# One-hot routing rows made by three instructions per group over pairs of 16-bit elements, with the late routing steps moved, in a recurrent layer followed by a mixture of experts

## The chip, the cores and the metric

The kernel runs on one core of one Trainium2 chip. The metric is the device time of one execution in microseconds. A core has a matrix engine (TensorE, "PE" in the profile, its weight loads "PEld"), a vector engine (VectorE, "DVE"), a scalar engine (ScalarE, "ACT"), a general engine (GpSimd, "POOL", which here also issues the gathers and scatters), and a queue engine (SyncE, "SP", which issues most plain DMAs). Each engine works through its own instructions in order and waits for the others through semaphores.

## The reference, cut to what matters

```python
# x: (2, 1024, 256), cond: (2, 256)
xW = einsum('ntd,dh->nth', x, Wx) + b
next_h = tanh(xw_t + prev_h @ Wh)              # scanned over 1024 tokens, from h = cond
...
logits = h_flat @ gate_w.T                     # 2048 tokens, 8 experts
top_v, top_i = top_k(logits, 2)                # two experts for each token
probs  = softmax(top_v)
...
hidden = silu(h @ wg_e.T) * (h @ wu_e.T)       # for each expert e
out   += combine[e] * (hidden @ wd_e.T)        # weights of the tokens that chose e
return x + out
```

The reference applies every expert to every token and multiplies by a weight that is zero for six of the eight. The kernel computes each expert only on the tokens that chose it, so it has to build, on the chip, a table that says which token stands in which place of which expert's list.

## The kernel before

**Three stages.** A recurrent stage (the loop over `s` from 8 to 63, L605) computes the hidden states. It cuts each of the two sequences into 64 chunks of 16 tokens and runs all 128 chunks side by side, each from 40 steps ahead of its first token; `df` holds by how much a chunk's start differs from the end of the chunk before, and a slower path (not taken here) is there for when that is too much. Steps 48 to 63 are the chunks' own tokens: each of them makes one tile of 128 tokens final. A routing stage runs inside the last steps of the recurrence and the first steps of the experts. An expert stage then takes ten units of work (an expert, or a part of an expert's tokens), each in eight steps. An expert step has a `front` (12 matrix products into `pgu_t`, L713), a `gate` (a Silu on ACT, then on DVE a product `g`, L721, then on ACT a copy `hh`, L732, and on DVE a remainder `hl`, L733, which lies beside `hh` in the same tile for a unit of 256 columns), and a `back` (products with `wd`, L875) for the step two before.

**Routing.** The 16 tiles are taken in four groups of four (`groups`; g0 to g3 below). For a group:

- `route_tile` (L333): for each tile, PE transposes the state and forms the logits (L340), and ACT copies them to `rows`.
- `route_max` (L343): for each tile, DVE finds the largest logits and their places (MAX8, then an index search).
- `route_choice` (L349): for the group, DVE makes `oh`, `sel` and `dl`, what was chosen and the difference of the two logits.
- `route_exp`: ACT takes an exponential of `dl`. It stands on ACT's queue in program order, so a tanh of the recurrence behind it waits with it.
- `route_position` (L376): PE counts, with `sel` of all groups so far, the place of each token in its expert's list (into `pos_ps`, L385).
- `route_code` (L389): DVE turns each of the eight (token, choice) columns of the group into a place: `v` is the block of 128 places, `m` the place inside it. POOL multiplies the probabilities in between.
- `route_onehot` (L413): DVE makes, for each of the eight columns, two rows of 128 values in 16-bit floats: `bv`, which holds the token's number (plus one) at column `v` and zero elsewhere, and `am`, which holds one at column `m`. Each row is one TENSOR_SCALAR instruction with a pointer to a scalar per partition (two pointers for `bv`): 16 instructions a group. The profile names both tiles `wd`, whose space they borrow, and gives their line as L50, the helper that keeps an engine's instructions in program order.
- `route_slots` (L422): PE multiplies `am` by `bv` and adds over all groups into `inv_ps`: the table of slots (L426).

`early_slots` (L459) reads the first two columns of the table once g0 and g1 are in, and POOL gathers two tiles of tokens for the first unit (from `rows_e`). `early_turn` transposes them on PE (L193), ACT makes `xhi`, DVE makes `xlo`, and the first front can start. `all_slots` (L471) reads the whole table once all groups are in, and POOL gathers two further tiles (the late gathers, from `rows_d`) for the second unit. They are turned in the expert step n = 6.

**What sets the order.** `at(step, f)` files a piece of work under a step, and `run(step)` emits all that is filed up to it, sorted by step and then by the order of filing. In the recurrence, `run(s - 0.5)` stands between the two halves of the eight products of step s, and `run(s)` at its end, after the tanh of ACT and after `seed(s + 2)`, which copies a summand to the accumulator of step s + 2 (one half on DVE, one on ACT in these steps). In expert step n, `run(64 + n + 0.15)` stands after the front, `+ 0.3` after the gate and `+ 0.6` after the back. `vec`, `act` and `pool` and all instructions of PE keep program order. `gated` and `halves` use `nc.vector` directly, and the compiler's planner may place those among the others.

In this listing the steps before stand in L542 to L583: the one-hot rows of g0 at 55 and 56, of g1 at 59, those of g2 and g3 split over 64.12 to 65.3; slots of g0 at 58, of g1 at 60.9, of g2 at 67.6, of g3 at 68.1; `early_slots` at 60.95 and `all_slots` at 68.15. A tile's maxima come one step after the tile.

Of the kernel before, what the change touches and what calls it, by code (L numbers as in the profile page):

```python
# [8 lines left out]
F32 = mybir.dt.float32  # L9
F32R = mybir.dt.float32r  # L10
F16 = mybir.dt.float16
I32 = mybir.dt.int32
U32 = mybir.dt.uint32
AF = mybir.ActivationFunctionType
ALU = mybir.AluOpType
# [4 lines left out]
P = 128  # L20
D = 256
NT = 2048
L = 16
R = 16
E = 8
# [7 lines left out]
ROW = D + E  # L33
S0 = 8
S16 = 28
GRP = 4
# [17 lines left out]
def rnn_moe(ctx, tc, xT, xrows, h0T, Wx, Wh, b, gw, W, out):  # L54
    nc = tc.nc
    pe = tc.keep_in_program_order
    vec, act, pool = (InOrder(tc, e) for e in (nc.vector, nc.scalar, nc.gpsimd))

    cst = ctx.enter_context(tc.tile_pool(name="cst", bufs=1))
    dram = ctx.enter_context(tc.tile_pool(name="dram", bufs=1, space=DRAM))  # L60
    ov = ctx.enter_context(tc.tile_pool(name="ov", bufs=1))
# [9 lines left out]
    iota_f = cst.tile([P, P], F32, name="iota_f")  # L71
    part_i = cst.tile([P, R], I32, name="part_i")
    tokp1 = cst.tile([P, R], F32, name="tokp1")
    iota16 = cst.tile([P, P], F16, name="iota16")
    trash = cst.tile([P, E * SPE // MT, MT], F32, name="trash").rearrange("p a b -> p (a b)")
    trash_i = cst.tile([P, E * SPE // MT, MT], I32, name="trash_i")
# [10 lines left out]
    def constants(part):  # L87
        if part == 0:
            vec.tensor_copy(iota_f, iota_i)
            vec.tensor_copy(tokp1, part_i)  # L90
            vec.tensor_scalar(ident, iota_f, 1.0, tokp1[:, 0:1], ALU.add, ALU.is_equal)
        elif part == 1:
            vec.tensor_scalar(upper, iota_f, 1.0, tokp1[:, 0:1], ALU.add, ALU.is_gt)
            vec.tensor_copy(ig[:, 0, 0:P], ident)
            vec.tensor_copy(ig[:, 1, E : P + E], ident)
            vec.tensor_copy(iota16, iota_f)
        elif part == 2:
            vec.tensor_copy(trash, trash_i.rearrange("p a b -> p (a b)"))
            vec.memset(ones16, 1.0)
            vec.tensor_scalar(base, iota_f[:, 0:E], float(SPE), None, ALU.mult)  # L100
        else:

            vec.tensor_scalar(keyc, iota_f[:, 0:E], FIRST - 0.5, 2.0**17, ALU.is_lt, ALU.mult)
            vec.scalar_tensor_tensor(keyc, iota_f[:, 0:E], float(8 * P * SPE + 1), keyc, ALU.mult, ALU.add)
# [15 lines left out]
    rt = wctx.enter_context(tc.tile_pool(name="rt", bufs=2))  # L120
# [24 lines left out]
    def flat(t):  # L145
        return t.rearrange("p a c -> p (a c)")
# [29 lines left out]
    hall = [flat(t).bitcast(F32).rearrange("p (r c) -> p r c", r=R) for t in early["gu_g"]]  # L176
# [25 lines left out]
    rp = c1.enter_context(tc.tile_pool(name="rp", bufs=1))  # L202
# [7 lines left out]
    zl = cst.tile([P, P], F32, name="zl")  # L210
    warm = rt.tile([P, 1], F32, name="warm")
# [10 lines left out]
    for c in range(4):  # L222
        constants(c)
# [31 lines left out]
    def bq(t):  # L255
        return t.rearrange("p (b q) -> p b q", b=2)
# [60 lines left out]
    slots = ov.tile([P, NO * NS], F32, name="slots")  # L317
# [6 lines left out]
    groups = []  # L324
    for g in range(R // GRP):
        o = (g % 2) * 4 * GRP * P
        gr = {"r0": g * GRP, "n": GRP}
# [61 lines left out]
    def route_code(gr, between=iter(())):  # L389
        n = gr["n"]  # L390
        rows = route_rows(gr, between)
        tmp = rt.tile([P, n, 2, E], F32, name="tmp")
        next(rows)
        vec.tensor_tensor(tmp, gr["oh"], pos_ps[:, 0:n, :].unsqueeze(2).to_broadcast([P, n, 2, E]), ALU.mult)
        code = rt.tile([P, n, 2], F32, name="code")
        next(rows)
        vec.tensor_reduce(code, tmp, AX.X, ALU.add)
        next(rows)
        big = 1.5 * 2.0**23 * P
        vv = rt.tile([P, n, 2], F32, name="vv")  # L400
        vec.tensor_scalar(vv, code, 0.5 - P / 2, big, ALU.add, ALU.add)
        next(rows, None)
        gr["v"] = v = rt.tile([P, 2 * n], F32, name="v")
        vec.tensor_scalar(v, vv.rearrange("p i c -> p (i c)"), -big, 1.0 / P, ALU.add, ALU.mult)
        gr["m"] = m = rt.tile([P, 2 * n], F32, name="m")
        next(rows, None)
        vec.scalar_tensor_tensor(m, v, -float(P), code.rearrange("p i c -> p (i c)"), ALU.mult, ALU.add)
        if gr["r0"] + n == NA:

            vec.tensor_scalar(gap, pos_ps[:, n, 0:1], -1.0 / P, float(ET), ALU.mult, ALU.add)  # L410
            vec.tensor_scalar(base[:, 0:1], gap, 0.0, None, ALU.max)

    def route_onehot(gr, part, js=range(2 * GRP)):  # L413

        for j in js:
            if part == 0:
                r = gr["r0"] + j // 2
                vec.tensor_scalar(gr["bv"][:, j, :], iota16, gr["v"][:, j : j + 1], tokp1[:, r : r + 1], ALU.is_equal, ALU.mult)
            else:
                vec.tensor_scalar(gr["am"][:, j, :], iota16, gr["m"][:, j : j + 1], None, ALU.is_equal)  # L420

    def route_slots(gr, i):  # L422
        for c in range(2):
# [90 lines left out]
    def first_weights(c, o):  # L514
# [6 lines left out]
            act.copy(hi[:, cc], raw[:, cc])  # L521
        (pool if c == 0 else vec).tensor_tensor(lo[:, cc], raw[:, cc], hi[:, cc].bitcast(F32), ALU.subtract)

    todo = {}

    def at(step, f, *args):
        todo.setdefault(step, []).append(lambda: f(*args))
# [12 lines left out]
    at(40, thresholds)  # L540

    for g, gr in enumerate(groups):  # L542
        t0 = 48 + gr["r0"] + gr["n"]
        for r in range(gr["r0"], gr["r0"] + gr["n"]):
            at(r + 49, route_tile, gr, r)
            at(min(r + 50, 64), route_max, gr, r)
        if g == R // GRP - 1:

            before = groups[g - 1]
            at(64, route_choice, gr)  # L550
            at(64.1, route_exp, gr)
            at(64.1, act.activation, warm, zl[:, 0:1], AF.Silu)
            at(64, rows_out, gr, ((0, P), (P + E, ROW)))
            at(64.12, route_position, gr)
            at(64.12, route_onehot, before, 0, range(4))
            at(64.12, route_code, gr, iter([lambda j=j: route_onehot(before, 0, range(j, j + 2)) for j in (4, 6)]))
            at(64.12, rows_out, gr, ((P, P + E),))
            at(64.3, route_onehot, before, 1)
            at(65.15, route_onehot, gr, 0)
            at(65.3, route_onehot, gr, 1)  # L560
            for i in range(gr["n"]):
                at(67.6, route_slots, before, i)
            for i in range(gr["n"]):
                at(68.1, route_slots, gr, i)
            continue
        at(t0 + 1, route_choice, gr)
        at(t0 + (1.5, 1.5, 1.9)[g], route_exp, gr)
        at(t0 + (2, 2, 2.5)[g], route_position, gr)
        at(t0 + (2, 2, 2.5)[g], route_code, gr)
        at(t0 + 1.5, rows_out, gr, ((0, P), (P + E, ROW)))  # L570
        at(t0 + (2, 2, 2.5)[g], rows_out, gr, ((P, P + E),))
        if g == 2:
            continue
        at(t0 + 3, route_onehot, gr, 0)
        at((t0 + 4, t0 + 3)[g], route_onehot, gr, 1)
        for i in range(gr["n"]):
            at(t0 + (6, 4.9)[g], route_slots, gr, i)
    at(60.95, early_slots)
    at(64, early_turn, 0)
    at(64, early_turn, 1)  # L580
    at(56, early_rows, 0, nc.sync)
    at(64.9, early_rows, 1, act)
    at(68.15, all_slots)  # L583

    inj = {}
    for s, q in ((15, 2), (31, 1), (47, 0)):
        t = rp.tile([P, 2, 2, 64], F16 if s + 1 < S16 else F32, name=f"inj{s}")
        inj[s] = (t, q)
        if q:
            nc.gpsimd.memset(t[:, :, :, 0:q], 0.0)  # L590
        for k in range(2):
            nc.gpsimd.tensor_copy(t[:, k, :, q], h0[:, k, :])
# [12 lines left out]
    for s in range(S0, 64):  # L605
# [7 lines left out]
        n, late = (s - S0 + 3) // 2, None  # L613
# [11 lines left out]
        if s in inj:  # L625
            t, q = inj[s]
# [4 lines left out]
        else:  # L631
            half = s + 1 < S16
            t = hp.tile([P, 2, 2, 64], F16 if half else F32, name="h16" if half else "h32")
# [4 lines left out]
        for j in range(2):  # L638
            x = bq(xw[s // 2][:, j, s % 2, :])[:, :, 0 : 64 - q0] if s == S0 else bq(acc[s % 2][j])[:, :, q0:64]
# [9 lines left out]
        n = (s - S0 + 6) // 2  # L649
# [1 line left out]
            x_split(n, (s - S0) % 2, act)  # L651
        run(s)

    df = ov.tile([P, 2, 2, 63], F32, name="df")
    for k in range(2):
        vec.tensor_tensor(df[:, k], inj[47][0][:, k, :, 1:64], bq(hall[k][:, L - 1, :])[:, :, 0:63], ALU.subtract)
    c1.close()

    okm = ov.tile([P, 1], F32, name="okm")
# [43 lines left out]
    with ExitStack() as c2:  # L703
# [216 lines left out]
        for n in range(len(steps)):  # L920
            i, s = steps[n]
            u = units[i]
            j = jobs.index(u.job)
            m = s + (NIC if i and units[i - 1].job is u.job else 0)
# [14 lines left out]
            if (j, m) in split_at:  # L939
                to, p = split_at.pop((j, m))  # L940
# [8 lines left out]
            if 2 <= n < len(steps) - NIC + TAIL + 2:  # L949
                v, t = done[n - 2]  # L950
# [180 lines left out]
```

## Time and profile before

| what | us |
|---|---|
| median of 3 runs | 395.32 (394.47 to 397.45) |
| the profiled execution, its own time | 392.31 |
| its span, first to last instruction | 390.5 |
| PE busy / PE weight loads busy | 371.0 / 349.5 |
| DVE / ACT / POOL busy | 232.5 / 200.5 / 119.9 |
| recurrence step 56 begins (PE) | 63.17 |
| first expert front begins (PE) | 81.11 |
| front of expert step 7 begins (PE) | 98.44 |

The granted clock of PE is 0.992 of full speed on average. Times inside the trace count from the start of the span. A line of the chain or of the timeline gives the start, the duration, the engine and the tile; "x8" means eight instructions merged. A line of the waits gives who waited for whom, the total in microseconds, how often, and the longest. A line of the groups gives busy time and the mean of one in nanoseconds, from issue to end: consecutive instructions overlap, so their starts lie closer together than that mean.

### The profile page before, as it was taken

How to read it: one execution, taken by the hardware profiler on the slowest of the kernel's cores; microseconds unless marked ns; L12 is line 12 of the kernel's file. 1: busy time of each engine (PE TensorE's matmuls, PEld its weight loads, DVE VectorE, ACT ScalarE, POOL GpSimd, SP SyncE). 2: the span in 40 equal slices, each digit the busy share in tenths (PEclk: the TensorE clock that was granted, in tenths of full speed). 3: DMA queues.
4: the chain of work that ended last, by engine and by line, in shares of the span. 5: the costliest groups of instructions: out<-in, count | busy, mean ns of one | idle time of the engine just before them, and what ended most of it. 6: DMA issues, size and time to landing. Idle time of an engine off the chain costs nothing.

```text
span 390.5 us, 7319 instructions
## 1 busy us (share of the span) xinstructions
PE 371.0 (95%) x2715; PEld 349.5 (90%) x2715; DVE 232.5 (60%) x619; ACT 200.5 (51%) x461; POOL 119.9 (31%) x124
## 2 busy tenths in 40 slices
PE   8899999988999999999999999999999999999990
PEld 7897898978998889999999999999989999999890
DVE  6676748988776565575537654575546656744410
ACT  3756666654664543665446553564454555535420
POOL 3790000213572501763041612432040015007041
PEclk9999999999999999999999999999999999999996
DMA  7943334441475343485233444345323307003122
GB/s 211 460 194 107 107 110 112 126 127 34 143 195 164 55 123 123 104 251 148 74 77 53 144 117 135 39 135 136 110 27 112 107 0 160 1 2 41 12 29 30
DMA packets 19291, 43.31 MB, mean 111 GB/s; under 512 B 4832, under 2 KB 14208, under 8 KB 16096
## 3 DMA queue, kind: packets, MB, share of 16 engines
q1 hardware_dynamic: 12432, 32.86, 25.2%
q0 software_dynamic: 6496, 9.09, 13.7%
q10 hardware_dynamic: 320, 0.80, 0.7%
q8 instruction: 24, 0.39, 0.4%
q14 instruction: 19, 0.16, 0.1%
HBM read 36.23 MB, written 10.22 MB: 119 GB/s over the span
## 4 chain that ended last, share of the span: by engine, by line
PE 82%; DVE 5%; DMA 4%; ACT 3%; POOL 2%; issue 2%; POOLq 0%; DVEq 0%
PE pgu_t L713 45%; PE yb L875 22%; PE pgu_t L612 8%; DVE wd L50 2%; PE ptr L286 2%; PE ptr L193 2%; POOL out_dram L454 2%; DMA gu_u<-in_xT_dram 1%; DMA wx<-in_Wx_dram 1%; PE pgu_t L875 1%; PE ptr L623 1%; ACT h L50 1%; ACT y L884 1%; DMA xg<-rows_e,gidx 1%; DMA xg<-rows_d,gidx 1%
## 5 line engine op out<-in xcount | busy, mean ns | idle before, releaser
L875 PE MATMUL yb<-wd,hh 128*128 128x256 f32 (+2 forms) x544 | 94.4, 284 | 1.0 <-ACT y L884 0.9
L875 PEld LDWEIGHTS yb<-wd,hh 128*128 128x128 f32 (+2 forms) x544 | 80.4, 185 | 3.5 <-ACT y L884 1.8
L721 DVE TENSOR_TENSOR g<-g,pgu_t 128x256 f32<-128x256 f32 (+5 forms) x96 | 49.9, 521 | 54.4 <-PE pgu_t L713 38.5
L732 ACT CAST hh<-g 128x256 fp32r<-128x256 f32 (+5 forms) x92 | 44.4, 484 | 68.9 <-DVE g L721 68.7
L454 POOL DMA_INDIRECT out_dram<-y,si x27 | 45.1, 1672 | 110.4 <-ACT y L884 105.5
L713 PE MATMUL pgu_t<-xhi,gu_g 128*128 128x256 f32 (+5 forms) x384 | 78.1, 325 | 0.6 <-ACT ex L50 0.6
L713 PE MATMUL pgu_t<-xhi,gu_u 128*128 128x256 f32 (+5 forms) x384 | 77.8, 324 | 0.0
L720 ACT ACTIVATE g<-pgu_t 128x256 f32<-128x256 f32 (+5 forms) x96 | 44.8, 466 | 53.1 <-PE pgu_t L713 49.6
L713 PEld LDWEIGHTS pgu_t<-xhi,gu_u 128*128 128x128 f32 x384 | 61.3, 188 | 4.3
L713 PEld LDWEIGHTS pgu_t<-xhi,gu_g 128*128 128x128 f32 x384 | 58.8, 189 | 3.1 <-issue 0.8
L875 PE MATMUL yb<-wd,hl 128*128 128x256 f32 (+1 forms) x176 | 49.5, 282 | 0.0
L447 POOL DMA_INDIRECT xg<-rows_d,gi x27 | 29.5, 1092 | 63.0 <-DVE cm L798 56.1
L733 DVE TENSOR_TENSOR hl<-g,hh 128x480 fp32r<-128x480 f32 (+4 forms) x52 | 30.9, 595 | 29.9 <-ACT hh L732 29.9
L713 PE MATMUL pgu_t<-xlo,gu_g 128*128 128x256 f32 (+5 forms) x192 | 46.6, 324 | 0.0
L713 PE MATMUL pgu_t<-xlo,gu_u 128*128 128x256 f32 (+5 forms) x192 | 46.5, 323 | 0.0
L713 PEld LDWEIGHTS pgu_t<-xlo,gu_u 128*128 128x128 f32 x192 | 32.5, 188 | 2.2
L713 PEld LDWEIGHTS pgu_t<-xlo,gu_g 128*128 128x128 f32 x192 | 32.5, 188 | 2.2
L875 PEld LDWEIGHTS yb<-wd,hl 128*128 128x128 f32 (+1 forms) x176 | 32.2, 183 | 0.1
L612 PE MATMUL pgu_t<-h,wh 128*128 128x128 f32 (+1 forms) x224 | 28.6, 266 | 1.4
L50 ACT ACTIVATE h<-pgu_t 128x128 f32<-128x128 f32 (+1 forms) x72 | 17.6, 276 | 13.9 <-PE pgu_t L612 8.7
L733 DVE TENSOR_TENSOR hh<-g,hh 128x256 fp32r<-128x256 f32 x40 | 16.8, 424 | 12.3 <-ACT hh L732 12.0
L612 PEld LDWEIGHTS pgu_t<-h,wh 128*128 128x128 f32 x152 | 18.4, 190 | 4.2 <-ACT h L50 3.3
(168 smaller groups left out, 471.5 us busy)
## 6 DMA issues: line engine op xcount, KB each, us to landing
raw<-in_W_dram SPq DMA_DIRECT2D x24, 1024.0 KB, 5.0
gu_u<-in_xT_dram SPq DMA_DIRECT2D x6, 256.0 KB, 5.9
rows_e<-gu_u SPq DMA_DIRECT2D x4, 256.0 KB, 2.7
rows_d<-rows_e SPq DMA_DIRECT2D x1, 528.0 KB, 4.9
rows_d<-rows_e ACTq DMA_DIRECT2D x1, 528.0 KB, 4.2
out_dram<-in_xrows_dram SPq DMA_DIRECT2D x1, 512.0 KB, 14.8
rows_d<-rows SPq DMA_DIRECT2D x2, 256.0 KB, 4.5
rows_d<-gu_u SPq DMA_DIRECT2D x2, 256.0 KB, 2.7
```

The costliest lines, as they stand in the source:

```text
L50: return lambda *a, **k: self.tc.keep_in_program_order(f(*a, **k))
L193: pe(nc.tensor.transpose(pt[:, m, j, :], tiles[i][:, k * (P + E) : k * (P + E) + P], ident))
L286: pe(nc.tensor.matmul(pt, lhsT=l, rhs=r, start=(i == 0), stop=(i == len(ops) - 1)))
L447: nc.gpsimd.indirect_dma_start(out=xg, out_offset=None, in_=rows[:, :], in_offset=bass.IndirectOffsetOnAxis(ap=idx, axis=0),)
L454: return nc.gpsimd.indirect_dma_start(out=out[:, :], out_offset=bass.IndirectOffsetOnAxis(ap=idx, axis=0), in_=y, in_offset=None, compute_ ...
L612: pe(nc.tensor.matmul(acc[s % 2][j], lhsT=w[:, k, j * P : (j + 1) * P], rhs=prev[k], start=False, stop=True, skip_group_check=True))
L713: pe(nc.tensor.matmul(pt, lhsT=a[i], rhs=b[j], start=(first and i + j + n == 0), stop=(j == 1 and n == len(lhs_rhs) - 1), skip_group_check ...
L720: nc.scalar.activation(g, pg, AF.Silu)
L721: nc.vector.tensor_tensor(g, g, pu, ALU.mult)
L732: nc.scalar.copy(hh, src)
L733: nc.vector.tensor_tensor(hl, src, hh.bitcast(F32), ALU.subtract)
L875: pe(nc.tensor.matmul(yt[0:w, :], lhsT=h[a][:, i * P : i * P + w], rhs=wd[b][:, ic, :], start=(ic == 0 and first and n == 0), stop=(ic == ...
```

## The change

The one-hot rows of a group are made by three TENSOR_TENSOR instructions over 1024 elements in place of 16 TENSOR_SCALAR instructions over 128. Part 0 compares a counter row (repeated for each of the eight columns) with `v`; part 1 multiplies the result in place by the token number; part 2 compares the counter row with `m`. So that an operand which is constant along a row still has two neighbouring 16-bit elements innermost, `v`, `m` and the token numbers are stored twice, side by side (`[.., 2]`, F16), and the constant is read as pairs with a step of zero over the 64 pairs of a row.

Work also changes places:

- g0: slots at 57.5 (between the halves of step 58) in place of 58; its second one-hot part moves from 56 to 55.
- g1: slots and `early_slots` at 61 in place of 60.9 and 60.95, so behind the tile of step 61 on PE.
- g2: its four maxima wait until 61.1, behind `early_slots` on DVE; choice at 62 (before 61), exponential 62.5 (61.9), position and code 63 (62.5), slots 66.6 (67.6). Its one-hot parts all lie within the code of g3 at 64.12.
- g3: its three one-hot parts at 65.3; slots and `all_slots` at 67.15 (68.1 and 68.15), one expert step earlier.
- `chunk_starts`: the two differences `df` of DVE, 126 elements wide each, come at 66.6 and not at the end of the recurrence; the tile they read (`inj47`) is kept longer.

```diff
+    tok16 = cst.tile([P, R, 2], F16, name="tok16")
...
+            vec.tensor_copy(tok16, tokp1.unsqueeze(2).to_broadcast([P, R, 2]))
...
-        gr["v"] = v = rt.tile([P, 2 * n], F32, name="v")
-        vec.tensor_scalar(v, vv.rearrange("p i c -> p (i c)"), -big, 1.0 / P, ALU.add, ALU.mult)
-        gr["m"] = m = rt.tile([P, 2 * n], F32, name="m")
+        gr["v"] = v = rt.tile([P, 2 * n, 2], F16, name="v")
+        twice = lambda t: t.rearrange("p i c -> p (i c)").unsqueeze(2).to_broadcast([P, 2 * n, 2])
+        vec.tensor_scalar(v, twice(vv), -big, 1.0 / P, ALU.add, ALU.mult)
+        gr["m"] = m = rt.tile([P, 2 * n, 2], F16, name="m")
         next(rows, None)
-        vec.scalar_tensor_tensor(m, v, -float(P), code.rearrange("p i c -> p (i c)"), ALU.mult, ALU.add)
+        vec.scalar_tensor_tensor(m, v, -float(P), twice(code), ALU.mult, ALU.add)
...
-    def route_onehot(gr, part, js=range(2 * GRP)):
-
-        for j in js:
-            if part == 0:
-                r = gr["r0"] + j // 2
-                vec.tensor_scalar(gr["bv"][:, j, :], iota16, gr["v"][:, j : j + 1], tokp1[:, r : r + 1], ALU.is_equal, ALU.mult)
-            else:
-                vec.tensor_scalar(gr["am"][:, j, :], iota16, gr["m"][:, j : j + 1], None, ALU.is_equal)
+    def route_onehot(gr, part):
+
+
+        n = gr["n"]
+        sh = [P, 2 * n, P // 2, 2]
+        pairs = lambda t: t.rearrange("p i (m t) -> p i m t", t=2)
+        if part == 1:
+            bv = gr["bv"].rearrange("p (i c) (m t) -> p i (c m) t", c=2, t=2)
+            tok = tok16[:, gr["r0"] : gr["r0"] + n, :].unsqueeze(2).to_broadcast([P, n, P, 2])
+            vec.tensor_tensor(bv, bv, tok, ALU.mult)
+            return
+        hot, x = ((gr["bv"], gr["v"]), None, (gr["am"], gr["m"]))[part]
+        count = iota16.rearrange("p (m t) -> p m t", t=2).unsqueeze(1).to_broadcast(sh)
+        vec.tensor_tensor(pairs(hot), count, x.unsqueeze(2).to_broadcast(sh), ALU.is_equal)
...
+    def chunk_starts():
+        for k in range(2):
+            vec.tensor_tensor(df[:, k], inj[47][0][:, k, :, 1:64], bq(hall[k][:, L - 1, :])[:, :, 0:63], ALU.subtract)
...
+            at(max(61.1, r + 50) if g == 2 else min(r + 50, 64), route_max, gr, r)
+
+    def group(g, choice, exp, position, rows, hot, slots):
+        gr = groups[g]
+        at(choice, route_choice, gr)
+        at(exp, route_exp, gr)
+        at(choice + 0.1, rows_out, gr, ((0, P), (P + E, ROW)))
+        at(position, route_position, gr)
+        at(position, route_code, gr, *rows)
+        at(position, rows_out, gr, ((P, P + E),))
+        for part, t in enumerate(hot):
+            at(t, route_onehot, gr, part)
         for i in range(gr["n"]):
-            at(t0 + (6, 4.9)[g], route_slots, gr, i)
-    at(60.95, early_slots)
+            at(slots, route_slots, gr, i)
+
+    group(0, 53, 53.5, 54, (), (55, 55, 56), 57.5)
+    group(1, 57, 57.5, 58, (), (59, 59, 59), 61)
+    at(61, early_slots)
+    group(2, 62, 62.5, 63, (), (), 66.6)
+
+    at(64.12, route_onehot, groups[2], 0)
+    group(3, 64, 64.1, 64.12, (iter([lambda p=p: route_onehot(groups[2], p) for p in (1, 2)]),), (65.3, 65.3, 65.3), 67.15)
...
-    at(68.15, all_slots)
+    at(67.15, all_slots)
+    at(66.6, chunk_starts)
...
-        t = rp.tile([P, 2, 2, 64], F16 if s + 1 < S16 else F32, name=f"inj{s}")
+        t = (rp if q else ov).tile([P, 2, 2, 64], F16 if s + 1 < S16 else F32, name=f"inj{s}")
```

More of the change, by code (lines that the diff above doesn't have):

```diff
@@ L522, in first_weights @@
         (pool if c == 0 else vec).tensor_tensor(lo[:, cc], raw[:, cc], hi[:, cc].bitcast(F32), ALU.subtract)
+    df = ov.tile([P, 2, 2, 63], F32, name="df")
+    def chunk_starts():
+        for k in range(2):
+            vec.tensor_tensor(df[:, k], inj[47][0][:, k, :, 1:64], bq(hall[k][:, L - 1, :])[:, :, 0:63], ALU.subtract)
     todo = {}
@@ L542, in rnn_moe @@
     for g, gr in enumerate(groups):
-        t0 = 48 + gr["r0"] + gr["n"]
         for r in range(gr["r0"], gr["r0"] + gr["n"]):
             at(r + 49, route_tile, gr, r)
[L546 to L575, printed above, removed]
-        for i in range(gr["n"]):
-            at(t0 + (6, 4.9)[g], route_slots, gr, i)
@@ L579, in rnn_moe @@
+    group(0, 53, 53.5, 54, (), (55, 55, 56), 57.5)
[4 more added lines that the diff above has]
+    group(3, 64, 64.1, 64.12, (iter([lambda p=p: route_onehot(groups[2], p) for p in (1, 2)]),), (65.3, 65.3, 65.3), 67.15)
+    at(64.1, act.activation, warm, zl[:, 0:1], AF.Silu)
     at(64, early_turn, 0)
@@ L652, in rnn_moe @@
         run(s)
-    df = ov.tile([P, 2, 2, 63], F32, name="df")
-    for k in range(2):
-        vec.tensor_tensor(df[:, k], inj[47][0][:, k, :, 1:64], bq(hall[k][:, L - 1, :])[:, :, 0:63], ALU.subtract)
     c1.close()
```

## The prediction

> **What bounds the kernel now.** I read the page first: PE is busy for 371.0 of 390.5 us. From 100 us on, the waits of PE show only 0.9 us (for ACT, two waits), so from there on the kernel is a stream of matrix products, and whatever is gained or lost earlier is passed on to the end. The change acts between 63 and 98 us. So I asked for the waits of PE in the window 56 to 100 us:
>
> ```profile
> PE yb L385 <- DVE sel L50: 1.0, 1, 1.0
> PE pgu_t L875 <- DVE hh L733: 0.9, 1, 0.9
> PE pgu_t L193 <- DMA xg<-rows_e,gidx: 0.8, 1, 0.8
> PE pgu_t L713 <- ACT ex L50: 0.6, 1, 0.6
> PE ptr L193 <- DMA xg<-rows_d,gidx: 0.4, 1, 0.4
> ```
>
> Five stalls, all tied to routing. To see what is late behind them I took the chain of waits in the same window:
>
> ```profile
> 63.41 1.77 DVE wd L50 x8
> 65.19 0.09 DVE mx L50
> ...
> 65.73 1.29 DVE wd L50 x8
> ...
> 71.11 3.07 DVE wd L50 x16
> ...
> 75.61 1.19 POOL xg L447
> 76.80 0.30 issue
> 77.10 2.97 DMA xg<-rows_e,gidx
> ...
> 85.93 3.09 DVE wd L50 x16
> 89.01 0.34 DVE hh L733
> ```
>
> The tile called wd with line L50 is the one-hot rows. They stand on the chain with 1.77 + 1.29 us for g0, 3.07 us for g1, and 3.09 us for a mix of g2 and g3. DVE works in order, so while it makes rows, the maxima, the summand of the next recurrence step and the remainder hl wait.
>
> The waits undercount, since some stalls fall between two products of one merged row. So I also counted from the timeline of PE. A step of the recurrence with its tile takes 1.36 us there (62.71 to 64.06, for example), 8 slot products about 0.46, a position about 0.4. Step 56 begins at 63.17, the first front at 81.11: 17.94 us. The work in it is 8 steps at 0.89 (7.12), 9 tiles at 0.47 (4.23), two groups of slots (0.92), two positions (0.8) and two turns at 0.23 (0.46): 13.5 us. The lost 4.4 us are (a) 1.1 before step 59 (starts 65.89 and 69.22, with 1.36 + 0.46 + 0.4 of work), (b) 1.1 before step 62 (71.93 to 74.87, with 1.36 + 0.46 of work), (c) 2.1 at the early gather, 78.5 to 81.1. After 81.11 there are (d) 1.1 us at 88.3 to 89.4, where the back waits for hl, and (e) 0.5 us at 96.8 to 97.3 for the late gather.
>
> The price of the old rows and of comparable whole instructions is in the groups of DVE by form:
>
> ```profile
> L50 DVE TENSOR_SCALAR wd<-iota,v,tokp 128x128 f16<-128x128 f16 x32 | 7.7, 308 | 0.0
> L50 DVE TENSOR_SCALAR wd<-iota,m 128x128 f16<-128x128 f16 x32 | 5.5, 245 | 0.0
> L50 DVE TENSOR_TENSOR wd<-raw,wd 128x512 fp32r<-128x512 f32 x4 | 2.8, 692 | 0.9 <-ACT wd L50 0.9
> ```
>
> and, from the window 90 to 260 us:
>
> ```profile
> L156 DVE TENSOR_TENSOR gu_g<-raw,gu_g 128x1024 fp32r<-128x1024 f32 x10 | 12.3, 1226 | 4.2 <-ACT gu_g L155 4.2
> ```
>
> [...] No 16-bit TENSOR_TENSOR is in this trace. [...]
>
> **The change part by part.** *New rows.* [...] estimated at 0.69 us by the price above, like the 512-element row. Starts of independent neighbours lie closer: the 512-element product after xlo starts 0.60 after it (98.54 to 99.14). Part 1 needs part 0's result, so it starts some 0.13 later. A group: 0.73 + 0.60 + 0.60 = 1.93 to its last issue, against 3.07, so 1.1 us less per group. Bounds: [...] at one per cycle 3 x 1.14 (97.04 to 98.18) + 0.1 = 3.5, which is 0.45 more than now. I take 1.93. The doubled v and m have 16 elements for 8[...]. tok16 is one copy, about 0.2 us, near 2.4 us, where DVE then waits 1.35 us for wx; without that cover 0.2.
>
> *g0 and step (a).* DVE: max, parts 0 and 1 from 63.7, a summand, a max, part 2, a summand, a max, choice: sel comes at 67.2 in place of 68.4. On PE the slots of g0 go between the halves of step 58 (am done by 66.3, PE there at 66.34), then the tile, then the position at 67.7, so sel is no longer late. ACT's exponential follows dl at 67.3, tanh of step 58 ends at 67.9. Step 59 starts at 68.1, not 69.22: stall (a) is gone, 1.1 us.
>
> *g1 and step (b).* Code ends at 69.6 (from 70.57), a summand 0.19, and no maxima of g2 between. Rows 69.8 to 71.8 in place of 71.02 to 74.18. The summand of step 62 then lands by 72.0. PE ends step 61 at 71.7, does the tile, then slots 72.2 to 72.6, and starts step 62 at 72.6, not 74.87: (b) is gone too. Moving the slots behind the tile costs the gather 0.4 us, and it is worth it only as cover for the rows.
>
> *The early gather (c).* The indices followed the slots (74.5) at 75.16, since two maxima and two summands stood ahead on DVE. Now nothing does: 72.7, so 2.4 earlier. POOL and the transfers (75.61 to 80.07) move along. Then PE waits for the second tile at 77.65, having arrived at about 77.0. That gap absorbs g2's deferral: four maxima (1.4 us), one more and the choice put sel at 75.5 and dl at 75.6. PE's position waits 0.2, and ACT's exponential holds the tanh of step 63 until 75.8, so its tile ends near 76.7, 0.7 ahead of the gather. Without that cover the deferral would cost some 1 us. xlo is ready 0.4 us later against the front than now, and is wanted 1.4 us into it. The first front would start at 78.7. But writes of g2's rows on SP's queue (two of 256 KB, issued when tile 11 is copied, 72.6 now, 71.2 then) and the copy of rows_e to rows_d (528 KB at 71.0) now lie closer ahead of the gather; they took 4.5 to 4.9 us to land. I allow 0.3: a start at 79.0, so 2.1 gained.
>
> *Experts, (d) and (e).* Around the code of g3, DVE does three parts of g2 (1.9 us) before the first g, where it did eight single rows (1.93), so the first back, whose hl was just in time (ended 85.93, back from 85.97), may wait 0.15. But then only g3's 1.9 us stand before the second hl, not 3.1: (d), 1.1 us, goes. The slots of g3 and all_slots come one step (2.1 us) earlier, and the step is no longer stretched by (d), so the gather starts about 3.7 us earlier against the front and is wanted 1.1 earlier: (e), 0.5 us, goes, with over 1 us to spare. ACT's copy of rows (issued 85.07, 4.2 to land) ends about when that POOL gather would start, so it may hold it by a few tenths, within the spare. chunk_starts moves 0.47 us of DVE from one place with slack to another. The slots are the same products as before.
>
> Sum: 2.1 + 1.1 + 0.5 - 0.15 = 3.55, or about 3.6 us. The profiled execution took 392.31 (span 390.5 and 1.8 around it), so it would take 388.7. It lies 3.0 below the median of the runs, 395.32; from there 391.7.
>
> **The rivals.** *One element per cycle.* [...] each instruction costs 1.14. [...] Then sel comes 0.45 late, the deferred maxima give about that back, and the front starts some 0.1 late; before the first hl stand 3.4 us in place of 1.93 (1.5 lost), before the second 0.45 more; (e) is still gained. 0.1 + 1.95 - 0.5 = 1.5 us slower: 396.8. Between 0.60 and 1.14 the effect goes from -3.6 to +1.5, so it decides at about 0.98 us an instruction.
>
> *The stall moves into the experts.* The planner may put all three parts of g3 ahead of the second g and the first hl, or the late gather waits for rows_d. For it: the first hl had 0.04 us of room. Against: there is 1.2 us less of rows to be hidden. It would keep the 2.1 and lose about 1.6 again: net 2.0 gained, 393.3.
>
> *The transfer decides.* If the early gather lands when it lands now, because it shares the engines with the 1.0 MB of row writes that are now closer, stalls (a) and (b) turn into a longer wait for it at L193, and only (d) and (e) count: 1.5 gained, 393.8. For it: DMA engines are two thirds busy at 78 to 82. Against: the same writes overlap it now.
>
> **How the numbers follow.** Likeliest: 0.64; stall in the experts 0.16; one per cycle 0.12; the transfer 0.08. The likeliest alone spans 389.4 to 393.3: the unknown in landing 0.6, in the overlap of rows 0.5, and a median of three that varies by about 1 us. With the second and fourth case the range reaches 395.3; I set 389.4 to 395.8, which leaves most of the one-per-cycle case out. One per cent, about what a measurement of this kernel can tell from no change, is 3.95 us. The likeliest case crosses it in half of its chance or a little more (0.36 in all), the milder ones stay within, and only one per cycle with a further stall gets beyond it on the other side (0.05). Faster 0.36, same 0.59, slower 0.05.
>
> **What would show it.** Three TENSOR_TENSOR of 128x1024 16-bit elements a group with a mean near 690 ns (1220 would be the first rival). Step 59 near 68.1, step 62 near 72.6, the first front near 79.0. No wait of L385 for sel; a wait of L193 for the early gather that stays; no wait of L875 for hh over 0.3; none of L193 for rows_d. From then on the same distance to the end as from 98.44 now. Wrong would be: a front before 78.3 or after 80, or a distance to the end that changes, for which I see no reason.

## The result and the profile after

The changed kernel takes 392.12 us (median of 12 runs, 391.52 to 395.11), the kernel before 394.49 (12 runs, 393.16 to 397.45): a ratio of 0.9938, 95% interval 0.9916 to 0.9961. The predicted time, 391.7, is 0.4 us off; the gain, 2.4 us, is smaller than the 3.6 of the sum. The profiled execution took 392.14 with a span of 390.4, almost what the first profile of the kernel before had (392.31 and 390.5), so the two pages hardly differ. Stage by stage they do.

The waits of PE between 52 and 100 us, in the changed kernel (in total, times, longest):

```profile
PE pgu_t L715 <- ACT xhi L200: 0.6, 1, 0.6
PE pgu_t L715 <- ACT xhi L50: 0.6, 1, 0.6
PE pgu_t L195 <- DMA xg<-rows_e,gidx: 0.5, 1, 0.5
PE pgu_t L877 <- issue: 0.5, 1, 0.5
PE yb L435 <- DVE wd L50: 0.2, 1, 0.2
```

The waits for sel, for hh or hl and for rows_d are gone, and the one for the early gather (rows_e) stays. New is the first line: L200 makes `xhi` of the second unit, and that unit's first front now waits for it. New but small is the last one: the slot products (L435), now earlier, wait 0.2 us for the rows. The 0.5 us of the fourth line, for which the profile shows no cause, end at 96.36, where the first line's wait begins soon after. The one-hot rows, in the groups of DVE by form:

```profile
L50 DVE TENSOR_TENSOR wd<-wd,tok 128x1024 f16<-128x1024 f16 x4 | 2.8, 689 | 0.1
L50 DVE TENSOR_TENSOR wd<-iota,m 128x1024 f16<-128x1024 f16 x4 | 2.7, 681 | 0.0
L50 DVE TENSOR_TENSOR wd<-iota,v 128x1024 f16<-128x1024 f16 x4 | 2.7, 680 | 0.0
```

8.2 us in place of 7.7 + 5.5 = 13.2. The chain of waits from 56 to 100 us:

```profile
67.02 0.23 PE yb L387 x10
67.26 1.00 PE pgu_t L617 x8
...
72.37 4.01 DMA xg<-rows_e,gidx
...
77.80 1.17 PE pgu_t L715 x8
...
96.50 0.38 ACT g L722
96.88 0.49 ACT xhi L200
97.41 1.93 PE pgu_t L715 x12
```

Up to the first front the rows of g0 and g1 have left the chain: PE makes g0's position (L387) and goes straight on with step 59 at 67.26. Behind the first front, from 80 to 86 us, the rows of g2 and g3 still stand on it (lines not shown). Near its end ACT stands on it, with the Silu of the gate of expert step 6 (into `g`; texts below call it the gate product on ScalarE) and `xhi` behind it. ACT's timeline shows why:

```profile
91.97 1.04 ACT L157 CAST gu_g<-raw 128x1024 fp32r<-128x1024 f32 x1
96.49 0.38 ACT L722 ACTIVATE g<-pgu_t 128x256 f32<-128x256 f32 x1 [3.48 <-PE pgu_t L715]
96.77 0.58 ACT L200 CAST xhi<-ptr 128x512 fp32r<-128x512 f32 x1
```

The bracket is the idle time ahead of the instruction: ACT is idle for 3.48 us from 93.01 on. But the last product of the front ahead of this Silu starts at 92.54 and is over, by the trace's modelled end, at 92.82. I call this idle time the hold. Where it comes, the second unit's `xhi` is late and its first front too.

To compare executions I take out how early each one started: all times below count from one tanh of ACT (58.60 us in the first profile of the kernel before, 57.72 in that of the changed kernel), the same instruction in every kernel, ahead of all that the change moves. "Front n" is the start of the products of expert step n, counted from 0; the last is front 95.

| profile | front 0 | front 7 | front 9 | front 17 | front 95 |
|---|---|---|---|---|---|
| before, first | 22.51 | 39.84 | 44.10 | 63.44 | 310.30 |
| changed, first | 20.08 | 36.09 | 42.17 | 62.47 | 311.02 |

The changed kernel leads by 3.75 us at front 7, loses 1.82 by front 9 (6.08 us from front 7 to front 9, against 4.26), and has lost all of it, and 0.7 us more, by front 95. In the second half of that loss are waits of the back products for `y`: after 100 us 2.4 us against 0.9 in the first profile of the kernel before.

```profile
PE yb L877 <- ACT y L886: 2.4, 4, 1.0
```

### The profile page after: what moved, and what is told of

It is laid out like the page before. It is cut to its first block, busy times and chain, and to the rows that moved or that the text cites. A ratio compares the mean times of both kernels' runs of the same rounds, so it can differ in the third digit from the quotient of the medians.

```text
span 390.4 us, 7267 instructions
## 1 busy us (share of the span) xinstructions
PE 371.9 (95%) x2715; PEld 349.9 (90%) x2715; DVE 228.1 (58%) x568; ACT 199.7 (51%) x461; POOL 119.8 (31%) x124
## 4 chain that ended last, share of the span: by engine, by line
PE 87%; DMA 3%; ACT 3%; POOL 2%; DVE 2%; issue 1%; ACTq 0%; POOLq 0%; DVEq 0%
PE pgu_t L715 46%; PE yb L877 22%; PE pgu_t L617 10%; PE ptr L288 2%; DMA gu_u<-in_xT_dram 2%; PE ptr L195 2%; POOL out_dram L463 2%; PE ptr L342 2%; PE pgu_t L877 1%; DMA xg<-rows_e,gidx 1%; PE ptr L628 1%; ACT y L886 1%; DVE wd L50 1%; ACT h L50 1%; PE ptr L877 1%
```

## The experiments

Open after the result: is the lead of front 7 lost because of the change (its rows, or its moves), or was one of the two profiles a rare one? Twelve runs were made, in three jobs, each job on one chip and a different one; the runs of the kernel before in the three had medians of 393.18, 391.39 and 393.73 us. The letters A and B belong to each job's own pair of theories.

**First job: each part alone.** The kernel before once more, for a second profile.

> The kernel before, unchanged, for a second profile. Its first profile took 392.31 us where the median of twelve runs is 394.49, so that profile may lack waits that most runs have. Theory A (the first profile was a lucky one): this one takes 394 to 395, with the five waits of the matrix engine between 56 and 100 us as in the first and a further 1 to 3 us of waits after 100 us. Theory B (nothing hidden): 392.3, with only 0.9 us of waits after 100 us.

It took 393.14 us, span 391.4, a little under the 394 to 395 of theory A. Its waits for `y` after 100 us are four, 2.5 us in all, like those of the changed kernel. So the y waits are no work of the change; it was the first profile of the kernel before (392.31 us, 2.2 under the median of the twelve runs of that kernel) that was unlike the rest.

The new rows in the old order: `route_onehot`, `tok16` and the doubled `v` and `m` of the change, all due times of the kernel before:

```diff
-            at(64.12, route_onehot, before, 0, range(4))
-            at(64.12, route_code, gr, iter([lambda j=j: route_onehot(before, 0, range(j, j + 2)) for j in (4, 6)]))
+            at(64.12, route_onehot, before, 0)
+            at(64.12, route_code, gr, iter([lambda: route_onehot(before, 1)]))
```

> The new rows in the old order: each group's rows by three instructions over pairs, everything filed where the kernel before has it. Theory A (rows and order each do a part): the wait for sel shrinks from 1.0 to about 0 to 0.3, g1's rows end 2.2 us earlier, the first front starts about 1.9 earlier (the maxima still stand ahead of the early gather's indices), the wait for hl near 88 falls from 1.1 to below 0.5, the late gather's wait of 0.5 stays: 2.0 to 2.8 us faster, a ratio of 0.993 to 0.995. Theory B (the order is what counts): within 0.5 us of before.

390.07 us, ratio 0.9904 (0.9882 to 0.9927): 3.1 us faster, more than the 2.0 to 2.8 of theory A. The new order with the old rows, the other half:

```diff
-        vec.tensor_tensor(pairs(hot), count, x.unsqueeze(2).to_broadcast(sh), ALU.is_equal)
+        for j in range(2 * GRP):
+            vec.tensor_scalar(gr["am"][:, j, :], iota16, gr["m"][:, j : j + 1], None, ALU.is_equal)
```

(and the like for the token rows.)

> The new order with the old rows: 16 single-row instructions a group (the eight bv rows where part 0 stands, the eight am rows where part 2 stands). Theory A: deferring g2's maxima and moving slots behind the tile wins back 0.5 to 1 us before the first front, all_slots one step earlier saves the 0.5 at the late gather, but eight bv rows and eight am rows of g2 (3.1 us against 1.9) now all stand ahead of the first gate and 3.1 of g3 ahead of the second hl, which costs 1 to 2 us: net between 0.5 faster and 1 slower, a ratio of 0.999 to 1.003. Theory B (the order is what counts): 2 us faster or more.

394.21 us, ratio 1.0022 (1.001 to 1.0035), as theory A has it. Here the hold is there as well, 2.83 us, while the new rows alone and the kernel before do not have it at this place. And the changed kernel with its constant operands read one element at a time, innermost step zero, in place of pairs:

```diff
-        count = iota16.rearrange("p (m t) -> p m t", t=2).unsqueeze(1).to_broadcast(sh)
-        vec.tensor_tensor(pairs(hot), count, x.unsqueeze(2).to_broadcast(sh), ALU.is_equal)
+        vec.tensor_tensor(hot, iota16.unsqueeze(1).to_broadcast(sh), x[:, :, 0:1].to_broadcast(sh), ALU.is_equal)
```

> The changed kernel with the operands that are constant along a row read as one element with an innermost step of zero, in place of pairs; same instructions, same order. Theory A [...]: each row instruction takes about 1220 ns in place of 685, a group 3.5 us in place of 1.93, and the kernel is 3 to 5 us slower than the changed one, 0.5 to 2 slower than before (ratio to before 1.001 to 1.005). Theory B (16-bit operands suffice): 685 ns and the time of the changed kernel.

396.67 us, ratio 1.008 (1.0062 to 1.0099), slower than the 1.001 to 1.005 of theory A. Groups of DVE by form in this kernel:

```profile
L50 DVE TENSOR_TENSOR wd<-wd,tok 128x1024 f16<-128x1024 f16 x4 | 4.9, 1221 | 0.1
L50 DVE TENSOR_TENSOR wd<-iota,v 128x1024 f16<-128x1024 f16 x4 | 4.9, 1214 | 0.0
```

and its largest wait of PE between 52 and 104 us:

```profile
PE yb L432 <- DVE wd L50: 4.1, 3, 2.3
```

So the pairs, not the merging, make the rows cheap: unpaired, a group's rows take 1.6 us more of DVE (3 x 1.21 against 3 x 0.68), and PE stands waiting for them at the slot products (L432). The hold came here too (1.56 us), but it delayed nothing: front 7 to front 9 took 4.26 us.

**Second job: is it the place of the late slots?** After the first job the hold stood in all profiles of the new order and in none of the old one. What differs ahead of it is that in the new order the second unit's gather has landed when PE comes to its transposes, so PE does not stop there. The next four kernels move that.

> The changed kernel once more, for a second profile. In its first profile ScalarE's gate product of the expert step 6 began 3.48 us after everything that it reads was done, and the second unit's first front was about 1.5 us late for it. Theory A (this hold belongs to the new order: there the two gathers of the second unit land before their transposes come, and all six gathers follow one another without a gap): the hold is there again, between 1.5 and 3.5 us, the fronts lose 1.2 to 1.8 us between the seventh and the ninth against the kernel before, ratio 0.993 to 0.995. Theory B (a chance of that one execution): no idle time over 1.5 us ahead of that product, and the ratio is 0.990 like that of the new rows alone.

388.1 us, ratio 0.992 (0.9894 to 0.9947). No hold, so theory A fell: the same place in ACT's timeline,

```profile
92.11 1.04 ACT L157 CAST gu_g<-raw 128x1024 fp32r<-128x1024 f32 x1
93.06 0.38 ACT L722 ACTIVATE g<-pgu_t 128x256 f32<-128x256 f32 x1
93.44 0.59 ACT L200 CAST xhi<-ptr 128x512 fp32r<-128x512 f32 x1
```

has no idle time at all, and the waits of PE between 52 and 100 us are the three below, with 0.8 us for `y` after that:

```profile
PE pgu_t L195 <- DMA xg<-rows_e,gidx: 0.6, 1, 0.6
PE pgu_t L715 <- ACT xhi L50: 0.6, 1, 0.6
PE yb L435 <- DVE wd L50: 0.2, 1, 0.2
```

This is the change without the hold. The late slots put back:

```diff
-    group(2, 62, 62.5, 63, (), (), 66.6)
+    group(2, 62, 62.5, 63, (), (), 67.6)
...
-    at(67.15, all_slots)
+    at(68.15, all_slots)
```

(and g3's slots to 68.1.)

> The changed kernel with only the slots of the groups g2 and g3 and all_slots put back to the places of the kernel before (67.6, 68.1 and 68.15), so that the second unit's gathers start about a step, 2.4 us, later. Theory A: no hold of the gate product of step 6; instead PE waits up to 0.7 us for a gather at its transposes, as in the kernel before. The lead of the earlier steps is kept: ratio 0.988 to 0.991, time 388.5 to 389.7 where the kernel before has 393.2. Theory B, or a hold that the moved chunk_starts makes: as the changed kernel, 0.993 to 0.995.

387.81 us, ratio 0.9899 (0.9874 to 0.9925). The reverse, the new rows in the old order with g2's slots at 66.6 and g3's and `all_slots` at 67.15:

> The kernel of the new rows in the old order, with only the slots of g2 and g3 and all_slots moved to the new places (66.6, 67.15, 67.15): the reverse of the run before. Theory A: the gathers land before the transposes, the hold comes, and of the 3.8 us that the rows alone brought 1.2 to 1.8 are lost: ratio 0.994 to 0.996. Theory B, or chunk_starts: no hold, ratio 0.989 to 0.991.

387.89 us, ratio 0.9905 (0.9879 to 0.9932). And `chunk_starts` back behind the recurrence:

```diff
-    at(66.6, chunk_starts)
...
+    chunk_starts()
     c1.close()
```

> The changed kernel with chunk_starts alone back behind the last recurrence step. Theory A: nothing changes for the gathers, the hold stays, ratio 0.992 to 0.996. If chunk_starts in the expert steps is what makes the loss: no hold, ratio 0.989 to 0.991.

388.33 us, ratio 0.9935 (0.9907 to 0.9962). None of these four profiles has a hold, in either order, so the job could not tell what place brings it. The theory that the order alone makes it has fallen: on this chip the same program goes without. What the job does show of the order is the wait for the late gather: with the late slots put back it returns,

```profile
PE ptr L195 <- DMA xg<-rows_d,gidx: 0.5, 1, 0.5
```

and with the early slots it is absent, in the old order as in the new. The intervals of the four ratios overlap; which of the four is fastest isn't shown.

**Third job: all parts side by side on one chip.** No new edits: the kernel before (a single run), the changed kernel, the new rows alone, the new order alone.

> The kernel before once more, so that the runs beside it have a profile of the kernel before from their own chip. Theory A (the hold of 1.5 to 3.5 us ahead of the gate product of expert step 6 is a matter of the chip or of the execution, and the change keeps its lead wherever it does not come): the distances to the end from the seventh front agree with those of the changed kernel in this job to within 0.3 us, unless a hold shows in one of the two. Theory B (the moves themselves cost time behind the seventh front): the changed kernel needs 0.7 us or more for the same distance without any hold.

> The changed kernel beside the new rows alone, on one chip. Theory A: both 0.990 to 0.994 and within 0.3% of each other; about 3 us under the kernel before. Theory B: 0.994, and the new rows alone 0.990.

> The new rows in the old order. Theory A: within 0.3% of the changed kernel beside it. Theory B: about 0.4% faster than the changed kernel. In both: a wait of 0.4 to 0.7 us for a gather of the second unit stays at its transposes, the sel wait of 1 us is gone.

> The new order with the old rows. Theory A: 0.998 to 1.001 where no hold shows, since the moves take the wait for the second unit's gather (0.4 us) away and make room, but leave VectorE as loaded as before. Theory B: 1.002 again, with the same 0.7 us or more lost behind the seventh front.

Measured: 393.08 us for the kernel before; 391.76 and 0.9951 (0.9937 to 0.9964) for the changed kernel; 389.55 and 0.9888 (0.9859 to 0.9918) for the rows alone; 393.35 and 0.9987 (0.9975 to 0.9999) for the order alone. The intervals of the first two ratios don't meet: on this chip the new rows in the old order beat the changed kernel, by about 0.6%. That fits neither theory A (both within 0.3%) nor the size in theory B (0.4%), and the order alone did a little better than theory B's 1.002, hold and all. Hold ahead of step 6: 3.35 us in the changed kernel, 2.82 in the order alone, none in the kernel before and the rows alone. In the changed kernel's timeline of PE it looks like this:

```profile
93.22 0.60 PE L195 MATMUL ptr<-ident,xg 128*128 128x128 f32 x4
...
95.79 0.87 PE L877 MATMUL pgu_t<-wd,hh 128*128 128x256 f32 x6
97.83 0.74 PE L715 MATMUL pgu_t<-xhi,gu_g 128*128 128x256 f32 x4 [1.17 <-ACT xhi L200]
```

PE goes from the front (ended near 93.4) through the transposes, the next front and a back without a stop, until at 96.66 it has nothing left but the front that needs `xhi`. The traces keep records of the counts of PE's semaphore: in the first profile of the kernel before it rises by one within 0.02 us of the end of each such piece of work. Here there is none between 91.26 and 96.83, then four within 0.27 us (96.83, 96.89, 96.92, 97.10), for the front of step 6, the transposes (two) and the front of step 7. In the second job's profile of the same kernel they come at 92.98, 93.31, 93.41 and 95.55, as each finishes. So by its records PE had done the work, and its counts came up to 3.5 us late.

The kernel before on this chip has the sel and hl waits of its first profile, in the waits of PE between 52 and 100 us,

```profile
PE pgu_t L875 <- DVE hh L733: 1.0, 1, 1.0
PE yb L385 <- DVE sel L50: 1.0, 1, 1.0
...
PE ptr L193 <- DMA xg<-rows_d,gidx: 0.4, 1, 0.4
```

and the rows alone have lost the first two and kept the third:

```profile
PE ptr L195 <- DMA xg<-rows_d,gidx: 0.4, 1, 0.4
```

From the tanh, as above (in the last column the hold ahead of step 6):

| profile | front 0 | front 7 | front 9 | front 17 | front 95 | hold |
|---|---|---|---|---|---|---|
| before, first job | 22.28 | 40.22 | 44.49 | 63.82 | 312.45 | 0 |
| before, third job | 22.49 | 40.22 | 44.48 | 64.11 | 312.15 | 0 |
| changed, second job | 20.11 | 36.11 | 40.38 | 59.68 | 306.51 | 0 |
| changed, third job | 20.19 | 36.20 | 42.14 | 62.32 | 310.37 | 3.35 |
| rows alone, first job | 20.56 | 36.68 | 40.94 | 60.57 | 308.90 | 0 |
| rows alone, third job | 20.18 | 36.33 | 40.60 | 61.64 | 309.67 | 0 |
| order alone, first job | 21.39 | 39.01 | 44.47 | 64.64 | 312.74 | 2.83 |
| order alone, third job | 21.45 | 38.96 | 44.37 | 64.58 | 312.68 | 2.82 |

Front 7 to front 9 takes 4.26 or 4.27 us in every line without a hold and 5.41 to 5.94 with one. Of the 4.0 to 4.1 us by which the changed kernel leads the kernel before at front 7, the rows alone bring 3.5 to 3.9 and the order alone 1.2 to 1.3; the two overlap.

The old order isn't free of late counts, though. In the third job's profile of the rows alone, ACT is idle for 2.90 us ahead of the Silu of step 7 (`remote` stands where the profile names nothing that ended the wait):

```profile
96.97 0.38 ACT L731 ACTIVATE g<-pgu_t 128x256 f32<-128x256 f32 x1 [2.90 <-remote]
```

In the first job's profile of the same kernel it is 1.06 us:

```profile
96.73 0.38 ACT L731 ACTIVATE g<-pgu_t 128x256 f32<-128x256 f32 x1 [1.06 <-PE pgu_t L724]
```

In the third job the front was over at 94.96 and its count is on record at 96.88, 1.9 us later; in the first job the two are 96.64 and 96.65. From front 9 to front 17 the third job's profile then takes 21.04 us, the first job's 19.63.

**What parts the profiles.** Over all of a trace the semaphore records divide the 14 profiles (the first two and the twelve) in two kinds. In five, the first of the kernel before and the four of the second job, each of PE's 488 counts is on record within 0.2 us of its product's end, and 2013 to 2016 landings of DMA are on record. In the other nine, 24 to 29 of PE's counts have no record within 0.2 us (they come up to 3.6 us late, or are missing), and only 1586 to 1664 landings are on record. The late or missing counts lie near 75, near 115 and near 168 us in all nine, old order and new; near 95 us (101 in the unpaired kernel) they lie in the five profiles of the new order and in the one of the rows alone above. From front 7 to the end of the span the five take 292.0 to 292.1 us, in both orders, and the nine 293.6 to 296.6. So holds, four y waits and missing records come together.

## Why the prediction was right, and where it failed

**The price of the rows: right.** Estimated 0.69 us, measured 0.680 to 0.689. The estimate put 1024 elements of 16 bits at the 692 ns that the trace before shows for 512 of 32 bits. That pairs run at twice the rate was an assumption: that trace has no 16-bit TENSOR_TENSOR to show it. "One element per cycle" stands in the prediction for the price of 1024 elements of 32 bits, 1226 ns and 1.14 us from start to start; the length of a cycle is shown by no trace. The unpaired kernel shows 1212 to 1221 ns: pairs with a step of zero over them took 0.56 of the time of a single element with a step of zero innermost. Part 1 started 0.71 us after part 0 where nothing stood between them (62.80 to 63.51, put at 0.73), part 2 0.60 after part 1 (84.43 to 85.03). The sum has no term for the doubled `v` and `m`, which take 246 and 186 ns in place of 213 and 163.

**(a), (b), (c): right.** I put step 59 at 68.1, step 62 at 72.6 and the first front at 79.0. The changed profile runs 0.88 us ahead from the tanh on; with that added its starts in the timeline of PE, 67.12, 71.72 and 77.80, are 68.00, 72.60 and 78.68. The gain at front 0 is 2.4 us for a predicted 2.1: the allowance of 0.3 for row writes close to the gather wasn't needed. From POOL's first gather instruction to the landing it took 4.01 us (72.37 to 76.38), against 4.46 before (75.61 to 80.07).

**(d) and (e): right in place, one term too small.** The hl wait is gone, and the gathers land before the transposes. Front 0 to front 7 is 1.32 us shorter (17.33 against 16.01) for 1.45 in the sum. The term for the first hl was too small, 0.15: the step from front 2 to front 3 is 0.63 us longer (2.11 to 2.74). That the place of the late slots frees PE of the rows_d wait, the second job shows in both directions.

**Sum at front 7: right.** 3.75 us against the first profile, 4.1 against the other two, for 3.55.

**"From then on the same distance to the end", with a changed distance "for which I see no reason": the step that failed.** In the profiles with complete records it is true to 0.1 us: from front 7 to the end of the span 292.0 us for the changed kernel in the second job, 292.1 in the first profile of the kernel before. In the first profile of the changed kernel it is 296.55. The 4.5 more are 1.82 between fronts 7 and 9, behind the hold; 0.97 at front 17, whose second `xhi` is late after the next turn (4.49 us from front 16 to 17 against 3.52); and 1.70 further on, where the y waits are. Only the first belongs to the new order. At front 17 the old order loses as well where records are missing (3.84 and 4.44 us in the third job's profiles of the kernel before and the rows alone), and y waits of 1.9 to 2.5 us are in all later profiles of the kernel before. The new order removed a stop of 0.4 us for the gather, and in its place came a late count of PE. I had costed the early landing as a gain with "over 1 us to spare" and had not asked what follows when PE runs through. The one profile that I had shows no late count.

**Why the time was right nonetheless: in part by luck.** The gain was put too high by 1.2 us (3.6 for 2.4). The starting point was too high as well, by 0.8: 395.32 was the median of three runs, that of twelve is 394.49. The two errors nearly cancel. Taking the sum from a profile 3.0 us below the median and carrying it over as a difference was sound as far as the stalls (a) to (e) go, since the y waits which that profile lacked lie behind them. Between two complete profiles, if of different jobs, the kernel does gain what the sum said, 3.8 us at front 95 (310.30 against 306.51).

**A slip in the chances.** A likeliest gain of 3.6 us lies under the 3.95 that one per cent is, so that case should cross it in less than half of its chance, not in "half or a little more".

**The rivals.** One element per cycle: not what happened, but the unpaired kernel is that case (1.21 to 1.22 us an instruction), and it lost 3.5 us (396.67 against 393.18), not 1.5. The largest piece that I had left out is PE's wait for rows at the slot products, 4.1 us in three waits: I had counted what the rows delay on DVE, and not that the moved slots now come before the slower rows are done. The stall in the experts: the right region, the wrong mechanism (no row of g3 is in the way). The transfer: didn't decide.

**Left open.** What holds PE's counts back. It isn't the new order as such: the same program shows it on one chip and not on another, and the old order has late counts too. The new order does add a place for it, near 95 us, in five of five profiles on the chips with missing records; the old order has it there in one of four. One candidate is the recording itself, since the counts are late where records are missing: 24 to 29 counts in the profiles with 1586 to 1664 landings, none in those with 2013 to 2016. That it did so here isn't shown and stays my guess: which of the two causes the other the traces don't say, and no run without a recording is there to compare. Late slots or moved `chunk_starts` on a chip that shows the hold weren't tried, nor the plain rows alone on the one that doesn't.

## What to carry to other kernels

Give a 16-bit operand that is constant along a row as stored pairs: here a comparison over eight rows (1024 elements) became one instruction of 0.68 us, where the constant read as single elements took 1.21. Look for the gain in the stage where it arises, from a marker ahead of the change, and over more than one profile: here the whole spans of the first two agreed to 0.1 us while one stage had gained 3.75. Before two profiles are compared, count their semaphore records: a profile with a fifth of the DMA landings missing was 1.5 to 4.5 us longer behind the change than a complete one, whatever the kernel. And test the parts alone: the rows brought nearly all of the gain at front 7, and on the one chip where all were run side by side they were faster without the moves made to match them.

## What the runs showed of the hardware that was not expected

- A product's count can be on record up to 3.6 us after the product, with PE working on (first profile of the changed kernel: over at 92.82, counted at 96.41), and ACT starts only then (96.49). In profiles without late counts it is 0.02 us at this place (over at 92.96, counted at 92.98, second job).
- Such late counts come with missing records. Five of 14 profiles have 2013 to 2016 DMA landings on record and no late count; nine have 1586 to 1664 and late counts in three or four stretches. With them go four y waits of 1.9 to 2.5 us in all, against two of 0.8 to 0.9.
- The second job's chip gave only complete profiles, the chips of the first and third jobs none. All kernels are faster on it (391.39 us for the kernel before, against 393.18 and 393.73); whether for this reason isn't shown.
